# Layer 1's routing: the last five strips settled as one batch beside the first tiles, six early batches, marks copied per strip, and the first plan in pieces

## The chip, the cores and the metric

The kernel runs on one core of a Trainium2 chip. The time is device microseconds of one execution; three executions of the kernel before are given with their median, and one more was taken with the hardware profiler. Engines are called PE (matmul), DVE (vector), ACT (scalar), POOL (GpSimd) and SP (the queue that issues most transfers).

## The reference

Two layers of a metaformer on an image of 2 x 256 channels x 56 x 56. In each layer a spatial mixer (layer 0: attention in 7 x 7 windows; layer 1: two 3 x 3 convolutions with ternary weights, each with batch normalization) is added to the image, and then a mixture of experts is added to every token. Cut to the part that is changed, layer 1's mixture is:

```python
logits = xf @ gate_w + gate_b                 # xf: 6272 tokens, layer-normed, 256 wide; 8 experts
probs = softmax(logits)
top2_vals, top2_idx = lax.top_k(probs, 2)
cw = zeros((N, 8)).at[arange(N)[:, None], top2_idx].add(top2_vals)
for e in range(8):                            # hidden width 512
    h = gelu(xf @ W1[e] + b1[e]); y = h @ W2[e] + b2[e]
    out = out + cw[:, e:e+1] * y
```

## The kernel before

The image is cut into 14 strips of 8 rows. A strip is 3 or 4 groups of 128 tokens (`groups_of`), 49 groups in all, and two strips are 7 groups. Layer 0 computes attention strip by strip, then its expert tiles; layer 1 computes the two convolutions, then the strips of its mixture, then its expert tiles, and at the end the sum of both experts of each token is written out.

**Rows and tiles.** Only the two chosen experts of a token are computed. `routing` gives every (token, expert) pair a place in a scratch tensor `xs` in DRAM, in which each expert has its own stretch of rows. A row is the normed token (256 words) and RW - 256 further words: `R_ID` is the number of the token's first output row, `R_EX` says which expert was its first choice. With these two marks the tile later finds where its results go. POOL scatters the rows, 128 per indirect DMA (L934), two per group: one for each choice. A tile is then 256 rows of one expert: SP loads the rows (`xg`, L1134) and the expert's weights (`w`, L1145, 1154 KB in layer 1), PE transposes the rows (`pt`, L1155), computes the hidden layer (`ph`, L1187) and the result (`py`, L1206), DVE adds the bias (`y`, L1216), and POOL scatters the results to `ys` (L1218). Half tiles of 128 rows take the remainders.

**A strip of layer 1.** `residual` loads `back`, forms x in DVE (L2213), relu in ACT (`nr`, L2216), transposes in PE (`pt`, L2226) and adds in DVE (L2230). `norm` takes the statistics (L744 to L754), scales in ACT (`u`, L767), transposes in PE (`pu`, L815), copies in ACT (`ut`, L818), and multiplies by the gate in PE (`pl`, L827); DVE adds the gate's bias (L836) and so has the logits `lgs`.

**A settling.** `settle(strips)` finds for all groups of a batch of strips the two largest logits (twice `first_max`, L862 to L866), counts (`hots` to `seen`, L887 to L892), has PE count the rows ahead of each within the batch (`rk`, L897 to L900), and turns that into places (`place`, `rowf`, `pos`, L909 to L916). It is a generator: each `yield` ends a step, and after the fourth each further step sends one group. In layer 1 a group that is sent before the tiles begin gets its marks on POOL first: a memset and two copies (L930 to L932). The strips after the ninth get theirs on DVE (L807, L808, L879).

**Plans.** `planning(part)` finds, by DVE on tables, the expert and first row of each tile (`where`), from counts that one matmul sums over the partitions (`counts`, L990, L992). Part 0 is made from the first nine strips alone (`FIRST[1]` is 9): 23 early tiles of 256 rows, whose rows are all known then. Parts 1 and 2, the remaining full and half tiles, are made while the early tiles run. A step of `planning` ends at each `yield`.

**Order.** Inside `manual_schedule` the order on SP, DVE, PE and ACT is the order in which the program emits. `all_strips` emits the strips in passes: in pass i strip i begins, strip i-1 goes on and strip i-2 ends; then the batch that ended is settled up to `rk`, and `send` finishes its places and scatters in the next pass. After the last strip it makes part 0 of the plan in one piece and starts the tiles' generator, which fetches the weights of three tiles; then the tiles begin with the rows of four. Beside the tiles `beside1` is called four times a tile, and each time takes one step of `rest`: of every four calls one goes to `sends` (groups held back), two to `settling` (the last two batches and then the other two plans), and one to nothing. The rows in `u` have eight buffers, `rk`, `pu` and `counts` share two PSUM banks in the strips, and beside the tiles `rk` and `counts` use a bank of `py`.

Of the kernel before, what the change touches and what calls it, by code (L numbers as in the profile page):

```python
# [20 lines left out]
P = 128  # L21
# [31 lines left out]
RW = C + 4  # L53
# [28 lines left out]
ROWS_AHEAD, AHEAD = 4, 3  # L82
UNITS = len(STRIPS) // 2
# [560 lines left out]
def metaformer(ctx: ExitStack, tc: tile.TileContext, a: dict, out: bass.AP, flag):  # L644
# [132 lines left out]
    def routing(layer, wp, tp, ps):  # L777
# [11 lines left out]
        chosen = wp.tile([P, NGR], F32, tag="chosen", name="chosen")  # L789
# [7 lines left out]
        def norm(i, src, late=False):  # L797
# [8 lines left out]
            if layer == 0 or i >= FIRST[1]:  # L806
                eng.memset(row[:, :, R_EX + 1 :], 0.0)  # L807
                eng.tensor_copy(row[:, :, R_ID], ids[:, g0 : g0 + ng])  # L808
# [32 lines left out]
        def settle(strips):  # L841
# [8 lines left out]
            def small(name, shape=(P, n, E), dt=F32):  # L850
                cap, size = max(n, NTT), int(np.prod(shape[1:]))
                t = tp.tile([P, size * cap // n], dt, tag=f"{name}_{cap}", name=name, bufs=1)
                t = t[:, :size]
                if len(shape) == 2:
                    return t
                if len(shape) == 3:
                    return t.rearrange("p (a b) -> p a b", b=shape[2])
                return t.rearrange("p (a b c) -> p a b c", b=shape[2], c=shape[3])
# [14 lines left out]
            at = [chosen[:, t0 : t0 + n], small("at", (P, n))]  # L873
            rest = small("rest")
            first_max(lg, m[0], hot[:, 0], at[0])
            if layer == 0 or strips[0] >= FIRST[1]:
                q = 0
                for u in us:
                    small_eng.tensor_copy(u[:, :, R_EX], at[0][:, q : q + u.shape[1]])  # L879
                    q += u.shape[1]  # L880
# [37 lines left out]
            for t in range(n):  # L918
                if layer == 0 or late:

                    with tc.issue_after(pace[-1]) if pace else nullcontext():
                        cast = nc.vector.tensor_copy(
                            pos[:, :, t0 + t : t0 + t + 1], rowf[:, :, t : t + 1]
                        )
                    if pace:
                        pace[:] = [cast.ins]
                if layer and not late:
                    u = at_of[t][0][:, at_of[t][1], :]
                    with tc.issue_after(spread[-1]) if spread else nullcontext():
                        nc.gpsimd.memset(u[:, R_EX + 1 :], 0.0)  # L930
                        nc.gpsimd.tensor_copy(u[:, R_ID : R_ID + 1], ids[:, t0 + t : t0 + t + 1])
                        nc.gpsimd.tensor_copy(u[:, R_EX : R_EX + 1], at[0][:, t : t + 1])  # L932
                for j in range(TOP):
                    w = nc.gpsimd.indirect_dma_start(  # L934
                        xs[:, :],
                        bass.IndirectOffsetOnAxis(ap=pos[:, j, t0 + t : t0 + t + 1], axis=0),
                        at_of[t][0][:, at_of[t][1], :],
                        None,
                    )
                    apart(f"rows{layer}", w)  # L940
                    if layer:
                        spread[:] = [w.ins]
                    if FIRST[layer] and strips[0] >= FIRST[layer]:

                        disjoint(w, f"late{layer}", f"early{layer}")
                yield
# [386 lines left out]
    BATCHES = [[0], [1], [2], [3], [4], [5, 6], [7, 8], [9, 10], [11, 12], [13]]  # L1333
# [510 lines left out]
    with mid:  # L1844
# [338 lines left out]
        with ExitStack() as both:  # L2183
# [54 lines left out]
            def send(steps, i):  # L2238

                if i >= FIRST[1]:  # L2240
                    if next(steps, steps) is not steps:
                        held.append(steps)
                else:
                    finish(steps)

            def all_strips():

                n = len(STRIPS)
                jobs = {}
                ready = iter(())  # L2250
                for i in range(n + 2):
# [3 lines left out]
                    send(ready, old - 1)  # L2255
# [9 lines left out]
                    steps = iter(())  # L2265
                    if old in jobs:
                        finish(jobs.pop(old))
                        for q in BATCHES[:-2]:
                            if q[-1] == old:
                                steps = settle(q)  # L2270
                    if i == n:
                        plan, n_early = tiles(0)
                        plans1.append(plan)
                        next(experts1)
                    for _ in range(3):
                        next(steps, None)
                    if old == 0:
                        finish(steps)
                    if young in jobs and i < n:
                        next(jobs[young])  # L2280
                    ready = steps
                send(ready, n - 1)
                return n_early

            def settling():

                for q in BATCHES[-2:]:
                    steps = settle(q)
                    for _ in range(4):
                        next(steps)  # L2290
                        yield
                    held.append(steps)
                yield from last_plans()

            def sends():

                at = 0
                while at < len(held):
                    yield from held[at]
                    at += 1  # L2300
# [8 lines left out]
            def rest():  # L2309
# [3 lines left out]
                while True:  # L2313
                    more = next(sending, sending) is not sending
                    yield
                    for _ in range(2):
                        more |= next(others, others) is not others
# [3 lines left out]
                    yield  # L2321
# [197 lines left out]
```

## Time and profile before

| | us |
|---|---|
| median of 3 runs (lowest, highest) | 1740.41 (1736.08, 1745.44) |
| the profiled execution | 1737.13 |
| its span, first to last instruction | 1735.3 |
| strips of layer 1's mixture | 1136 to 1262 |
| first transposition of tile 0 | 1278.2 |
| last products of the last tile | 1670 |

In the profile a group of instructions is named by line, engine and tile, as "PE pl L827"; `out<-in` are the program's names. The chain that ended last is followed back from the last instruction, at each step to what released it. In the order of instructions, a bracket at the end of a line is the idle time of that engine before it and what ended it. PEclk is the clock that PE was granted, as a share of full speed. "SPq" is SP's own queue: L1143 and L1129 read a number of the plan into a register, L1145 issues a weight load.

### The profile page before, as it was taken

The numbers are of one execution on the slowest core, as the hardware profiler recorded it, in microseconds if no ns is written. First come the engines' busy times: TensorE is split into PE (matmuls) and PEld (weight loads), VectorE is DVE, ScalarE is ACT, GpSimd is POOL, SyncE is SP. The second block draws the span as 40 slices with busy tenths as digits, with TensorE's granted clock in tenths as the row PEclk, the third lists the DMA queues.
The fourth block names the chain that finished last, engine by engine and source line by source line (L and its number), as shares of the span: only waits on it lengthen the run. The fifth ranks groups of instructions, "written<-read, shape, count | busy, mean of one in ns | idle before, by whom it ended". The sixth has DMA issues, their size and how long they took to land. (4 is left out here: it accounts for less than half of the span.)

```text
span 1735.3 us, 25573 instructions
## 1 busy us (share of the span) xinstructions
PE 1507.6 (87%) x8445; PEld 1176.0 (68%) x8445; DVE 957.5 (55%) x2620; ACT 692.9 (40%) x1419; POOL 636.8 (37%) x728
## 2 busy tenths in 40 slices
PE   5999998999878788894989879957769999999964
PEld 3555565556557667783768768746658888888852
DVE  3456667466635335885999888777622212111136
ACT  2544443444323324544444263235423334343323
POOL 2111436235333653552333323427715542222210
PEclk9999999999879999996999989955579999999975
DMA  7112334112257769794441000024357777888858
GB/s 241 42 64 90 111 102 145 60 62 80 80 181 248 249 203 322 258 331 176 170 170 70 1 1 0 10 65 141 126 198 274 271 258 262 282 288 288 293 198 317
DMA packets 94157, 291.78 MB, mean 168 GB/s; under 512 B 20151, under 2 KB 35611, under 8 KB 84928
## 3 DMA queue, kind: packets, MB, share of 16 engines
q1 hardware_dynamic: 70384, 231.82, 40.3%
q0 software_dynamic: 19824, 51.82, 7.9%
q10 hardware_dynamic: 3808, 6.42, 1.0%
q8 instruction: 69, 1.13, 0.3%
q14 instruction: 72, 0.59, 0.1%
HBM read 218.55 MB, written 74.20 MB: 169 GB/s over the span
## 5 line engine op out<-in xcount | busy, mean ns | idle before, releaser
L1187 PE MATMUL ph<-ut,w 128*128 128x256 f32 (+1 forms) x1472 | 311.8, 363 | 18.5 <-DMA w<-in_L_experts 10.0
L1216 DVE TENSOR_TENSOR y<-py,w 128x512 f32<-128x512 f32 (+1 forms) x120 | 76.8, 640 | 412.5 <-PE py L1206 341.4
L1206 PE MATMUL py<-w,h 128*128 128x256 f32 x1288 | 300.5, 381 | 3.4 <-DVE y L1216 2.5
L1187 PEld LDWEIGHTS ph<-ut,w 128*128 128x128 f32 x1472 | 251.4, 195 | 49.6 <-DMA w<-in_L_experts 10.3
L1206 PEld LDWEIGHTS py<-w,h 128*128 128x128 f32 x1288 | 244.5, 192 | 37.1 <-DVE y L1216 2.9
L934 POOL DMA_INDIRECT xs<-u,pos x196 | 194.0, 990 | 127.9 <-issue 43.1
L1218 POOL DMA_INDIRECT ys<-y,dest x136 | 137.0, 1008 | 233.0 <-DVE dest L1162 100.4
L1194 ACT ACTIVATE h<-ph,w 128x256 f32<-128x256 f32 (+1 forms) x368 | 162.6, 448 | 119.0 <-PE ph L1187 91.5
L1597 ACT ACTIVATE ex<-sc 112x476 f32<-112x476 f32 (+3 forms) x224 | 116.9, 573 | 177.6 <-PE sc L1587 169.8
L1159 ACT COPY ut<-pt 128x512 f32<-128x512 f32 (+1 forms) x120 | 65.1, 543 | 293.1 <-PE pt L1155 258.2
L1928 PE MATMUL pc<-lo,wq 128*128 128x448 f32 x336 | 131.8, 394 | 5.7 <-DVE lo L1903 5.4
L1617 DVE TENSOR_TENSOR acc<-av,acc 128x238 f32<-128x238 f32 (+3 forms) x224 | 88.1, 408 | 82.9 <-PE av L1607 74.7
L1928 PE MATMUL pc<-hi,wq 128*128 128x448 f32 x336 | 131.0, 392 | 2.5 <-DVE x L1950 1.9
L1607 PE MATMUL av<-ex,vals 112*64 112x238 f32 (+3 forms) x896 | 126.9, 407 | 4.0 <-DVE acc L1617 4.0
L1218 POOL DMA_INDIRECT ys<-y,to x81 | 81.7, 1009 | 121.9 <-DVE dest L1162 63.4
L2071 PE MATMUL pc<-hi,wq 128*128 128x448 f32 (+1 forms) x288 | 102.5, 366 | 18.1 <-ACT hi L2038 9.4
L1578 PE MATMUL sc<-q_im,keys 32*112 32x238 f32 (+3 forms) x896 | 99.2, 423 | 7.9 <-ACT ex L1597 7.8
L2071 PE MATMUL pc<-lo,wq 128*128 128x448 f32 (+1 forms) x288 | 101.8, 363 | 0.2 <-DVE lo L2039 0.2
L1155 PE MATMUL pt<-ident,xg 128*128 128x128 f32 x434 | 71.2, 285 | 33.6 <-DMA xg<-xs 25.5
L1901 POOL TENSOR_TENSOR v<-pad 128x928 f32<-128x928 f32 (+1 forms) x28 | 56.7, 2035 | 103.5 <-ACT pad L1884 59.5
L1607 PEld LDWEIGHTS av<-ex,vals 112*64 112x64 f32 x896 | 57.3, 143 | 53.5 <-issue 30.0
L1155 PEld LDWEIGHTS pt<-ident,xg 128*128 128x128 f32 x434 | 56.5, 148 | 48.8 <-DMA xg<-xs 22.5
(278 smaller groups left out, 2474.5 us busy)
## 6 DMA issues: line engine op xcount, KB each, us to landing
w<-in_L_experts SPq DMA_DIRECT2D x64, 1154.0 KB
w<-in_L_experts SPq DMA_DIRECT2D x56, 641.0 KB
xg<-xs SPq DMA_DIRECT2D x97, 260.0 KB
acc<-in_fresh SPq DMA_DIRECT2D x14, 896.0 KB
got<-ys SPq DMA_DIRECT2D x21, 512.0 KB
got<-ys SPq DMA_DIRECT2D x7, 1024.0 KB
xt<-in_x_tok SPq DMA_DIRECT2D x14, 448.0 KB
rec<-shares SPq DMA_DIRECT2D x28, 224.0 KB
```

The lines of the kernel that those rows point to most:

```text
L934: w = nc.gpsimd.indirect_dma_start(xs[:, :], bass.IndirectOffsetOnAxis(ap=pos[:, j, t0 + t : t0 + t + 1], axis=0), at_of[t][0][:, at_of[t] ...
L1155: nc.tensor.transpose(pt[:, k, i * P : (i + 1) * P], d["xg"][:, i, k * P : (k + 1) * P], ident)
L1187: nc.tensor.matmul(ph[:, :g], w1[:, k, f * P : (f + 1) * P], d["ut"][:, k, :g], start=k == 0, stop=k == KC - 1,)
L1194: nc.scalar.activation(d["h"][:, f, :g], ph[:, :g], AF.Gelu, bias=b1[:, f : f + 1])
L1206: nc.tensor.matmul(py[:, i, :], d["h"][:, f, i * P : (i + 1) * P], w2[:, f, :], start=f == 0, stop=f == NF - 1,)
L1218: o = nc.gpsimd.indirect_dma_start(ys[:, :], bass.IndirectOffsetOnAxis(ap=d["to"][:, i : i + 1], axis=0), y[:, i, :], None, bounds_check=T ...
L1578: nc.tensor.matmul(sc[h // 2][:, h % 2, :nq], keys[g][p, c, tx * TT : (tx + 1) * TT], q_im[p, c, r0:r1, c0:c1], start=True, stop=False,)
L1597: nc.scalar.activation(e[:, :, :nq], sc[j][:, :, :nq], AF.Exp, scale=HD**-0.5)
L1607: nc.tensor.matmul(av[VW * i : VW * (i + 1), :nq], vals[g % 3][:, tx, 2 * c + j, 2 * i : 2 * i + 2, :].rearrange("p a d -> p (a d)"), ex[j ...
L1617: added = nc.vector.tensor_tensor(d, av[:, :nq].rearrange("p (h w) -> p h w", w=c1 - c0), d, ALU.add)
L1928: nc.tensor.matmul(pc[:, :NT], wq[:, k, c, dx * C + o * P : dx * C + (o + 1) * P], part[:, :, k, dx : dx + W], start=m == 0, stop=m == 2 * ...
L2071: nc.tensor.matmul(pc[:, : 2 * ns * W], wq[:, k, c, dx * C + o * P : dx * C + (o + 1) * P], part[:, : 2 * ns, k, dx : dx + W], start=m == ...
```

## The change

- `RW` falls by two words; a row now has 258. `chosen` becomes the second column of a table `marks`, whose first column is filled once from `ids`; in both layers POOL copies both marks for a whole strip in one instruction. Memsets of the two spare words are gone, and so are the copies for the late strips on DVE.
- The batches of layer 1 were [0], [1], [2], [3], [4], [5,6], [7,8], [9,10], [11,12], [13]; the last two were settled beside the tiles. They become [0], [1], [2], [3,4], [5,6], [7,8], and one batch of 18 groups, [9..13], beside the tiles.
- A batch that ends with strip 5 or later is settled in three parts: `first_max` twice in its own pass, the counting and `rk` in the next, places and scatters in the one after.
- Part 0 of the plan is made in pieces of three steps from pass 11 on, and the weights of three tiles are fetched as soon as it is done.
- Beside the tiles the order of steps is one of eight calls: three for sends, three for settling and plans, two for nothing.

```diff
@@ -50,7 +50,7 @@
 NFULL = (TOP * N - E * (G - 1)) // G
 NHALF = (TOP * N + E * (P - 1)) // P - 2 * NFULL
 ROWS = NREG * G
-RW = C + 4
+RW = C + 2
 R_ID, R_EX = C, C + 1
 FAR = 1 << 20
 NEVER = -3e38
@@ -80,6 +80,7 @@
 EARLY = tuple(max(0, (TOP * P * groups_of(n)[0] - E * (G - 1)) // G) for n in FIRST)
 X_FIRST = 3
 ROWS_AHEAD, AHEAD = 4, 3
+PLAN_AT = 11
 UNITS = len(STRIPS) // 2
 FOURS = ((0, 1), (2, 3, 4, 5), (6, 7, 8, 9), (10, 11, 12, 13))
 COMPS4 = 6
@@ -786,7 +787,8 @@
         most = wp.tile([P, TOP, NGR], F32, tag="most", name="most")
         pos = wp.tile([P, TOP, NGR], I32, tag="pos", name="pos")
         wgt = rt.tile([P, TOP, NGR], F32, tag="wgt", name="wgt", bufs=2)
-        chosen = wp.tile([P, NGR], F32, tag="chosen", name="chosen")
+        marks = wp.tile([P, NGR, 2], F32, tag="marks", name="marks")
+        nc.gpsimd.tensor_copy(marks[:, :, 0], ids)
         seen = wp.tile([P, E], F32, tag="seen", name="seen")
         nc.vector.memset(seen, 0.0)
         seen_b4 = wp.tile([P, E], BF16, tag="seen_b4", name="seen_b4")
@@ -803,9 +805,6 @@
             row = tp.tile([P, NTT, RW], F32, tag="u", name="u", bufs=U_BUFS[layer])
             row = rows[i] = row[:, :ng]
             u = row[:, :, :C]
-            if layer == 0 or i >= FIRST[1]:
-                eng.memset(row[:, :, R_EX + 1 :], 0.0)
-                eng.tensor_copy(row[:, :, R_ID], ids[:, g0 : g0 + ng])
             scaled(u, src, rstd, nmr)
             yield
             ut = tp.tile([P, KC, NTT * P], F32, tag="ut", name="ut", bufs=1)
@@ -838,7 +837,7 @@
                 nc.vector.tensor_copy(lg, pl)
             yield
 
-        def settle(strips):
+        def settle(strips, pool=None):
 
 
             t0 = groups_of(strips[0])[0]
@@ -849,7 +848,9 @@
 
             def small(name, shape=(P, n, E), dt=F32):
                 cap, size = max(n, NTT), int(np.prod(shape[1:]))
-                t = tp.tile([P, size * cap // n], dt, tag=f"{name}_{cap}", name=name, bufs=1)
+                t = (pool or tp).tile(
+                    [P, size * cap // n], dt, tag=f"{name}_{cap}", name=name, bufs=1
+                )
                 t = t[:, :size]
                 if len(shape) == 2:
                     return t
@@ -870,13 +871,13 @@
             lg = lgs[:, t0 : t0 + n, :]
             m = [most[:, j, t0 : t0 + n] for j in range(TOP)]
             hot = small("hot", (P, TOP, n, E))
-            at = [chosen[:, t0 : t0 + n], small("at", (P, n))]
+            at = [marks[:, t0 : t0 + n, 1], small("at", (P, n))]
             rest = small("rest")
             first_max(lg, m[0], hot[:, 0], at[0])
-            if layer == 0 or strips[0] >= FIRST[1]:
-                q = 0
+            if layer == 0:
+                q = t0
                 for u in us:
-                    small_eng.tensor_copy(u[:, :, R_EX], at[0][:, q : q + u.shape[1]])
+                    nc.gpsimd.tensor_copy(u[:, :, R_ID:], marks[:, q : q + u.shape[1]])
                     q += u.shape[1]
             nc.vector.scalar_tensor_tensor(rest, hot[:, 0], NEVER, lg, ALU.mult, ALU.add)
             yield
@@ -924,12 +925,12 @@
                         )
                     if pace:
                         pace[:] = [cast.ins]
-                if layer and not late:
-                    u = at_of[t][0][:, at_of[t][1], :]
+                if layer and at_of[t][1] == 0:
+                    u = at_of[t][0]
                     with tc.issue_after(spread[-1]) if spread else nullcontext():
-                        nc.gpsimd.memset(u[:, R_EX + 1 :], 0.0)
-                        nc.gpsimd.tensor_copy(u[:, R_ID : R_ID + 1], ids[:, t0 + t : t0 + t + 1])
-                        nc.gpsimd.tensor_copy(u[:, R_EX : R_EX + 1], at[0][:, t : t + 1])
+                        nc.gpsimd.tensor_copy(
+                            u[:, :, R_ID:], marks[:, t0 + t : t0 + t + u.shape[1]]
+                        )
                 for j in range(TOP):
                     w = nc.gpsimd.indirect_dma_start(
                         xs[:, :],
@@ -1330,7 +1331,7 @@
             except StopIteration as end:
                 return end.value
 
-    BATCHES = [[0], [1], [2], [3], [4], [5, 6], [7, 8], [9, 10], [11, 12], [13]]
+    BATCHES = [[0], [1], [2], [3, 4], [5, 6], [7, 8], [9, 10, 11, 12, 13]]
 
 
     ys = [dram.tile([TOP * N, C], F32, tag=f"ys{i}", name=f"ys{i}", bufs=1) for i in range(2)]
@@ -2235,24 +2236,18 @@
 
             norm, settle, tiles, planning, gates, wgt1, _, sent = routing(1, wp, tp, ps)
 
-            def send(steps, i):
-
-                if i >= FIRST[1]:
-                    if next(steps, steps) is not steps:
-                        held.append(steps)
-                else:
-                    finish(steps)
-
             def all_strips():
 
                 n = len(STRIPS)
-                jobs = {}
-                ready = iter(())
+                jobs, steps = {}, iter(())
+                ready, early = iter(()), None
                 for i in range(n + 2):
                     young, old = i - 1, i - 2
                     if young in jobs:
                         next(jobs[young])
-                    send(ready, old - 1)
+                    finish(ready)
+                    next(steps, None)
+                    ready, steps = steps, iter(())
                     if young == 0:
                         next(jobs[young])
                     if i < n:
@@ -2262,42 +2257,46 @@
                         next(jobs[young])
                     if i == n:
                         next(jobs[young])
-                    steps = iter(())
                     if old in jobs:
                         finish(jobs.pop(old))
-                        for q in BATCHES[:-2]:
+                        for q in BATCHES[:-1]:
                             if q[-1] == old:
                                 steps = settle(q)
-                    if i == n:
-                        plan, n_early = tiles(0)
-                        plans1.append(plan)
-                        next(experts1)
-                    for _ in range(3):
-                        next(steps, None)
-                    if old == 0:
-                        finish(steps)
+                                next(steps)
+                                next(steps)
+                                if old < 5:
+                                    next(steps)
+                                    ready, steps = steps, iter(())
+                                if old == 0:
+                                    finish(ready)
+                    if i == PLAN_AT:
+                        early = planning(0)
+                    if i >= PLAN_AT and not plans1:
+                        try:
+                            for _ in range(3):
+                                next(early)
+                        except StopIteration as end:
+                            plan, n_early = end.value
+                            plans1.append(plan)
+                            next(experts1)
                     if young in jobs and i < n:
                         next(jobs[young])
-                    ready = steps
-                send(ready, n - 1)
                 return n_early
 
             def settling():
 
-                for q in BATCHES[-2:]:
-                    steps = settle(q)
-                    for _ in range(4):
-                        next(steps)
-                        yield
-                    held.append(steps)
+                steps = settle(BATCHES[-1], tp1)
+                for _ in range(4):
+                    next(steps)
+                    yield
+                held.append(steps)
                 yield from last_plans()
 
             def sends():
 
-                at = 0
-                while at < len(held):
-                    yield from held[at]
-                    at += 1
+                while not held:
+                    yield
+                yield from held[0]
 
             def last_plans():
 
@@ -2311,14 +2310,13 @@
                 yield
                 sending, others = sends(), settling()
                 while True:
-                    more = next(sending, sending) is not sending
-                    yield
-                    for _ in range(2):
-                        more |= next(others, others) is not others
+                    more = False
+                    for it in (sending, others, others, None, sending, others, sending, None):
+                        if it:
+                            more |= next(it, it) is not it
                         yield
                     if not more:
                         return
-                    yield
 
             plans1, held = [], []
             gating = gates()
```

## The prediction

> **What bounds the kernel now.** I read the page first, then the busy time by stages, then the chain that ended last around the edit, then the order of instructions on POOL, PE and DVE there.
>
> ```profile
> span 1735.3 us, 25573 instructions
> PE 1507.6 (87%) x8445; PEld 1176.0 (68%) x8445; DVE 957.5 (55%) x2620; ACT 692.9 (40%) x1419; POOL 636.8 (37%) x728
> ```
>
> The profiled execution took 1737.13 us: 1.8 us lie around the span. The median shown is 1740.41, 3.3 above it. 87% of PE is a mean over stages; the edit is in layer 1's strips and in the start of its tiles.
>
> ```profile
> core 0: us, PE busy (x) PEld busy (x) DVE busy (x) ACT busy (x) POOL busy (x), PEclk, DMA share, GB/s
> 1136.00:1262.00 126.00, 93.97 (x439) 80.36 (x439) 90.56 (x362) 60.53 (x119) 74.31 (x153) 0.53 0.36 114
> 1262.00:1278.00 16.00, 0.04 (x2) 0.00 (x0) 4.25 (x21) 0.00 (x0) 0.00 (x0) 0.50 0.64 252
> 1278.00:1300.00 22.00, 21.81 (x109) 19.02 (x110) 4.76 (x25) 9.32 (x17) 5.85 (x6) 0.91 0.56 207
> 1300.00:1440.00 140.00, 140.00 (x691) 123.16 (x690) 33.54 (x139) 49.33 (x99) 69.04 (x70) 1.00 0.76 262
> ```
>
> To be seen: 126 us of strips in which no engine is full and PE runs at half clock; 16 us in which PE does nothing; then tiles with PE 100% busy. A microsecond saved before 1278 is kept through the PE-bound tiles.
>
> ```profile
> 1258.86 3.16 PE pl L827 x14
> 1262.09 0.18 DVE counts L992
> ...
> 1265.89 0.12 SPq L1143
> ...
> 1266.48 0.35 SPq L1145
> ...
> 1269.08 0.34 SPq L1145
> ...
> 1270.33 7.81 DMA xg<-xs
> 1278.19 1.97 PE pt L1155 x8
> 1280.15 4.51 PE ph L1187 x16
> ...
> 1285.10 3.46 PE ph L1187 x16
> ```
>
> The gap in order: the plan on DVE (1262.1 to 1265.9), three weight loads of 1154 KB issued from 1266.5 to 1269.4, then the rows of tile 0, issued 1270.3 and landed 1278.1. From the first weight issue to that landing are 11.7 us for 3 x 1154 + 260 KB, about 320 GB/s.
>
> ```profile
> 1250.59 0.11 POOL L930 MEMSET u<- 128x2 f32 x1
> 1250.63 0.19 POOL L931 COPY u<-ids 128x1 f32<-128x1 f32 x1
> 1250.75 0.18 POOL L932 COPY u<-chosen 128x1 f32<-128x1 f32 x1
> 1251.21 0.99 POOL L934 DMA_INDIRECT xs<-u,pos  x1 [0.28 <-issue]
> 1252.51 0.96 POOL L934 DMA_INDIRECT xs<-u,pos  x1 [0.30 <-issue]
> ```
>
> One group on POOL: 2.88 us from one memset to the next, of which two scatters with their pauses are 2.55. POOL is nearly continuous from 1169 and finishes the early rows at 1253.5, so today the scatter is covered by the strips.
>
> ```profile
> 1224.71 0.23 PE L897 MATMUL rk<-hots,before_w 128*128 128x56 bf16 x1 [1.79 <-DVE hots L887]
> 1226.79 1.12 PE L815 MATMUL pu<-ident,u 128*128 128x128 f32 x4 [0.68 <-issue]
> 1233.63 1.23 DVE L2230 TENSOR_TENSOR x<-pt,back 128x1024 f32<-128x1024 f32 x1 [1.66 <-PE pt L2226]
> ```
>
> A pair of strips takes 16.6 to 18.6 us (starts of the four-group L2230: 1164.1, 1182.7, 1199.8, 1216.5, 1233.6, 1251.0). PE waits for a settling's `hots`, DVE for PE's `pt`: a chain over both.
>
> **The change, part by part.** I call the pass that begins with L2230 of strip i-1 "pass i"; passes 10, 12, 14 begin at 1216.5, 1233.6, 1251.0.
>
> (1) Fewer settlings in the strips. [3] goes into [4]: pass 5 lasted 10.0 us (1172.7 to 1182.7) with DVE's settling after L836; without it PE's `pt`, done at 1181.0, ends the pass: -1.5, and -0.2 in pass 6 (DVE loses four place instructions, 0.8, and gains 0.6 by larger ones). [9,10] leaves pass 12: 16 DVE instructions, 3.7 us, counted in (4).
>
> (2) Settlings [5,6] and [7,8] in pieces. `hots` to `seen` (4 instructions, 0.85) and `rk` go to the next pass, `place` to `pos` (0.9) to the one after. Pass 8 loses 0.85 on DVE and PE its 1.8 wait; pass 9 gains the 0.85 ahead of L2213, but its PE work starts earlier with two free `pu` banks: -1.5 for the pair. In pass 10 `place` now sits before L2213, where DVE is the chain: +0.9, which cancels the 0.85: the pair 10-11 gains 0.9.
>
> (3) The plan in pieces, passes 11 to 13. 20 DVE instructions, 3.8 us in the chain above. The order of the changed kernel shows the price of the first piece: `counts` (L990) stands on PE behind `pt` of strip 11, and DVE's L992 to L1024 stand before L2230 of that strip. So DVE waits for `counts`, and L2230 with all behind it starts 2.4 us after `pt` instead of at once; PE's next `pu` takes the bank of `counts` and waits 0.3. Costs 2.4, no cover; (2) less (3) makes the pair 10-11 1.5 longer. The second piece (4 instructions, 1.1) takes part of the place of [9,10]; the third (1.6) fits in the 1.66 in which DVE waited for PE; without that cover it costs 1.6.
>
> (4) Pass 12: DVE 3.1 (L2230, statistics) + 0.9 (`place`) + 1.6 + 0.2 + 1.1 = 6.9; PE's `pt` then ends it at 7.9 instead of 8.8; pass 13 7.9 instead of 8.5: -1.5. Sum at pass 14: -1.7 - 1.5 + 1.5 - 1.5 = -3.2: it begins at 1247.8 and the strips, 11 us later, end near 1258.7.
>
> (5) POOL. Memset and two copies per group go; one copy per strip stays, about 0.45 with its pause. A batch of seven groups: 7 x 2.55 + 0.45 = 18.3. [5,6] starts 4.4 after pass 10 (1213.3), at 1217.7, ends 1236.0. [7,8] is a pass later: 4.1 after pass 12 (1231.9), at 1236.2; ends 1254.5, a microsecond later than before in spite of the fewer instructions. From the end of the last scatter to the rows' issue I take 2.2 (the chain's scatter of 1218.19 landed 3.15 after its start) to 4.1 (layer 0: 489.7 to 493.8): issue at 1256.7 to 1258.6. Layer 0's first rows took 2.8 from issue to use: 1259.5 to 1261.4.
>
> (6) Weights. `where` is ready just before pass 14, so the loads issue at about 1248. Queued on SP before them are only the strips' loads of `back`, the last of them done by then; behind them only the rows. The trace's layer 0 would have the rows 2.8 after their issue. The Trainium skill, "DMA: Bandwidth & Descriptors", section "Queues, rings and completion order", says descriptors of one issuing queue are consumed in ring order on each engine: the rows cannot pass the weights. By that rule 1248 + 11.7 = 1259.7, plus 2 for the 0.6 MB of scatter in the same time at 320 GB/s: 1261.5. Both ways end near 1261.4; I take this for tile 0, against 1278.2: -16.8. The PE gap is then 2.7 us.
>
> (7) In the tiles. One settling of 18 groups for two of 7 and 4: 19 `rk` matmuls on the bound PE instead of 13, wider; from the rows of 0.2 and their overlap I estimate +0.5 to +1.5, take +1. DVE (24% busy from 1300 to 1440) covers its 24 wider instructions; if not, `y` is late, and `py` has two banks. POOL has 2 ys and on average 3 xs a tile, 5 x 1.29 = 6.4 of 7.35 us; PE sees it only when the five `y` buffers are used up. The sends end near tile 15, before rows of the late plan are fetched at tile 19.
>
> (8) Rows of 258 instead of 260 words, layer 0's memsets and copies gone from POOL and DVE, some early DVE and SP instructions reordered, Exp one tile earlier: 0, hidden by attention and PE-bound tiles; bounds -2 and +2, as POOL loses some 28 x 0.15 and a swapped load at the start may come later.
>
> Sum: -16.8 + 1 = -15.8, about -16: 1721 on the profiled execution's own time, 1724.4 on the median's.
>
> **A rule against the gain.** PE is at 0.50 in the strips, and tile 0's `ph` took 4.51 against 3.46. "TensorE: Matmul & The Clock Gate", Part 1, says half clock holds until PE has been busy through a window of about 3.4 us. By the trace alone the 1.05 warm-up is paid as before; by the rule a 2.7 us gap may keep what the strips have, which is half clock, so the same. But if fewer stalls in the strips let a window fill, `pl` (6.2 of each pair) and the transposes would halve: up to 3 us per pair over some three pairs, -9. No run shows it; I take 0 and keep -9 as the lower end.
>
> **Rivals.**
> A, 60%: as above, -11 to -20.
> B, 20%: the gap becomes a transfer wait. Weights and scatter slow each other; if the last scatters land 6 to 9 us later (their 0.6 MB and the 3.5 MB at 200 to 250 GB/s, rates that other stages show, in place of 320), tile 0 starts near 1269: -8, 1732. For it: nothing in the trace shows this mix. Against: 320 GB/s was reached.
> C, 10%: the clock rule's upside, or POOL sooner: -20 to -27, about 1717.
> D, 7%: slower. The row of xs shrinks to 1032 bytes, no longer a multiple of 16. If writing and reading such rows cost three times as much, the later tiles, where DMA runs at 0.84 share and 288 GB/s, become transfer-bound: there a full and a half tile in 11.1 us move 390 KB of rows; 780 KB more at 288 GB/s is 2.7 us per pair, less 1.8 of spare, over 18 pairs +16, and as much at tile 0 and in layer 0: 1752. It decides from about double cost. Against: rows of 1040 also start off most boundaries.
> E, 3%: the start waits for something not seen (a buffer or bank freed only at the strips' end): the gap stays, -2.
>
> **How the numbers follow.** 0.5% (8.7 us) is about what a measurement of this kernel can tell from no change. Faster by more: A, C and nearly half of B, 0.79. Within: the rest of B, E, 0.13. Slower: D and a small rest, 0.08. Range: A with its bounds, most of B and the edge of C, with the 4 us by which runs of before scatter: 1714 to 1736.
>
> **What would show it.** Tile 0's `pt` (L1155) near 1261 with 2 to 5 us of PE idle before it; weights issued near 1248; L2230 of strip 11 late by about 2.4 with DVE waiting for `counts`; POOL's last early scatter near 1254.5, without memsets; tiles at 7.35 us as before. Wrong if tile 0 starts after 1268 (B, E), if PEclk in the strips rises above 0.6 (C), or if tiles grow beyond 7.4 us (D).

## The result, and the profile after

The changed kernel takes 1746.41 us in the median of 22 runs (1739.43 to 1755.85), the kernel before 1740.57 us on the same chip (22 runs): a ratio of 1.0039, 95% interval [1.0024, 1.0054]. It is slower by 0.4%, where 16 us less had been forecast. The profiled execution took 1753.02 us, near the upper end of the runs.

The page of the changed kernel:

```profile
span 1751.2 us, 25389 instructions
PE 1512.9 (86%) x8442; PEld 1180.2 (67%) x8442; DVE 948.4 (54%) x2546; ACT 690.0 (39%) x1419; POOL 621.9 (36%) x627
```

DVE and POOL have less to do, as planned (POOL 101 instructions fewer). The busy time by stages, which answers to the table of before:

```profile
core 0: us, PE busy (x) PEld busy (x) DVE busy (x) ACT busy (x) POOL busy (x), PEclk, DMA share, GB/s
1148.50:1293.40 144.90, 91.67 (x425) 79.64 (x425) 85.14 (x328) 58.89 (x117) 63.13 (x71) 0.51 0.39 129
1293.40:1315.40 22.00, 22.00 (x115) 19.17 (x116) 5.50 (x21) 9.30 (x17) 2.25 (x3) 0.89 0.48 166
1315.40:1455.40 140.00, 139.14 (x684) 122.29 (x683) 30.94 (x121) 47.70 (x99) 73.31 (x78) 1.00 0.77 262
```

There is no row for a gap any more: the strips are followed at once by tiles with PE full. But the strips take 144.9 us, with PE busy for no more time than before. On PE, at the seam:

```profile
1290.35 3.16 PE L826 MATMUL pl<-gate,ut 128*128 128x8 f32 x14 [0.26 <-ACT ut L817]
1293.36 1.95 PE L1156 MATMUL pt<-ident,xg 128*128 128x128 f32 x8
1295.13 1.22 PE L1188 MATMUL ph<-ut,w 128*128 128x256 f32 x2
```

The last logits (`pl`) run into tile 0's `pt` with no idle time; before, 16.15 us lay between. Those 16 us were gained, and more than 16 were lost inside the strips. To compare runs I count from the first L2231 (before: L2230) of layer 1's strips, since that point itself moves from run to run: 1139.8 before, 1148.5 here, and 1147.8 in a kernel below (e3) whose code up to there is that of before. From it, tile 0 starts at 138.4 us before and at 144.9 now. That difference, 6.5 us, agrees with the 0.4% by which the medians differ.

Where the strips lose it, the waits between 1148 and 1294 us tell (engine and line, who ended the wait; total, times, longest):

```profile
ACT ut L817 <- remote: 28.2, 6, 9.4
...
DVE counts L993 <- remote: 9.8, 1, 9.8
...
DVE x L2231 <- remote: 7.9, 2, 4.5
```

"remote" stands where the signal that ended a wait has no recorded instruction ending next to it. The strips before have no such wait. All are waits for PE, whose instructions stand in the trace microseconds earlier. One of them in order of time:

```profile
1247.35 2.35 PE L2227 MATMUL pt<-ident,nr 128*128 128x128 f32 x8 [1.11 <-issue]
...
1248.27 0.96 POOL L935 DMA_INDIRECT xs<-u,pos  x1 [0.30 <-issue]
1249.23 0.20 POOL L931 COPY u<-marks 128x6 f32<-128x6 f32 x1
...
1249.49 0.21 PE L991 MATMUL counts<-seen_b,all_w 128*128 128x8 bf16 x1
1249.71 0.98 POOL L935 DMA_INDIRECT xs<-u,pos  x1 [0.28 <-issue]
...
1256.05 0.96 POOL L935 DMA_INDIRECT xs<-u,pos  x1 [0.30 <-issue]
1257.00 0.21 POOL L931 COPY u<-marks 128x8 f32<-128x8 f32 x1
1257.74 0.17 DVE L993 COPY counts<-counts 128x8 f32<-128x8 f32 x1 [9.79 <-remote]
...
1258.06 0.88 PE L814 MATMUL pu<-ident,u 128*128 128x128 f32 x3 [8.35 <-DVE counts L993]
```

PE's eight `pt` and the `counts` behind them would end at 1249.7 by their usual durations; PE's signals, which the trace records by themselves, come at 1257.68 and 1257.72. DVE, which needs `counts`, stands still for 9.8 us, and PE then for 8.35. POOL meanwhile scatters on, one every 1.27 us, from 1239.2 to 1257.0, and the hold-up ends with POOL's last scatter. So it is with every run of 14 scatters in the strips: POOL scatters from 1177.6 to 1195.7, from 1208.3 to 1226.4, from 1239.2 to 1257.0 and from 1265.0 to 1283.0, and the waits of this kind (for L2231, `ut` and `counts`) end at 1194.0 and 1196.8, at 1225.4 and 1228.3, at 1257.7, and at 1279.4 to 1285.0. The first wait of each group begins 8 to 11 us after the run's start; PE's signals then come singly, and the last of the waits ends 0.7 to 2 us after the run.

### The profile page after: what moved, and what is told of

Same layout as the page of the kernel before. It is cut to its first block, busy times and chain, and to the rows that moved or that the text cites. A ratio compares the mean times of both kernels' runs of the same rounds, so it can differ in the third digit from the quotient of the medians.

```text
span 1751.2 us, 25389 instructions
## 1 busy us (share of the span) xinstructions
PE 1512.9 (86%) x8442; PEld 1180.2 (67%) x8442; DVE 948.4 (54%) x2546; ACT 690.0 (39%) x1419; POOL 621.9 (36%) x627
## 5 line engine op out<-in xcount | busy, mean ns | idle before, releaser
L826 PE MATMUL pl<-gate,ut 128*128 128x8 f32 x392 | 68.3, 304 | 25.7 <-ACT ut L817 13.9
L826 PEld LDWEIGHTS pl<-gate,ut 128*128 128x128 f32 x392 | 65.7, 254 | 34.3 <-ACT ut L817 17.2
```

Of the source, the lines that this page charges most:

```text
L826: nc.tensor.matmul(pl[:, t, :], ut[:, k, t * P : (t + 1) * P], gate[:, k, :], start=k == 0, stop=k == KC - 1,)
```

## The experiments

Times are medians, each beside the kernel before on the same chip; the ratio is that of the comparison and need not be the quotient of the two medians. Five sets of runs were made. In the first and the last the kernel before took 1740.1 and 1743.7 us, as in the result; in the second, third and fourth 1720.2, 1720.8 and 1722.1. They ran on chips 14, 10, 13, 13 and 8; the chip of the result is not on record.

| kernel | us | before | ratio, 95% interval |
|---|---|---|---|
| e1_paced | 1732.1 | 1740.1 | 0.9934 [0.9902, 0.9966] |
| e2_before_rows258 | 1742.9 | 1740.1 | 1.0002 [0.9982, 1.0021] |
| e3_before_dense | 1758.6 | 1740.1 | 1.0078 [1.0042, 1.0114] |
| e4_copy_per_group | 1734.3 | 1740.1 | 0.9964 [0.9939, 0.9989] |
| b1_paced_early | 1709.7 | 1720.2 | 0.9931 [0.9906, 0.9957] |
| b2_paced | 1709.6 | 1720.2 | 0.9933 [0.9905, 0.9961] |
| b3_paced_late_plan | 1714.3 | 1720.2 | 0.9969 [0.9952, 0.9986] |
| e5_half_rows | 1708.3 | 1720.2 | 0.9913 [0.9890, 0.9937] |
| after_2 (the changed kernel) | 1709.0 | 1720.8 | 0.9925 [0.9900, 0.9950] |
| e5_half_rows_2 | 1705.5 | 1720.8 | 0.9914 [0.9886, 0.9942] |
| b2_paced_2 | 1706.9 | 1720.8 | 0.9920 [0.9900, 0.9940] |
| after_3 (the changed kernel) | 1700.7 | 1722.1 | 0.9871 [0.9843, 0.9899] |
| e5_half_rows_3 | 1702.4 | 1722.1 | 0.9898 [0.9865, 0.9931] |
| b2_paced_3 | 1710.0 | 1722.1 | 0.9919 [0.9888, 0.9949] |
| b5_paced_both | 1707.7 | 1722.1 | 0.9923 [0.9897, 0.9948] |
| e5_half_rows_4 | 1750.8 | 1743.7 | 1.0043 [1.0007, 1.0079] |
| b5_paced_both_4 | 1730.5 | 1743.7 | 0.9922 [0.9894, 0.9950] |

**First set: the pace of the scatters, the rows, or the order.** Of the changed kernel, only the pauses on POOL are put back (e1), or a shorter one (e4); of the kernel before, only the row width (e2) or only the missing pauses (e3) is changed.

e1:

```diff
-                if layer and at_of[t][1] == 0:
+                if layer and not late:
+                    u = at_of[t][0][:, at_of[t][1], :]
...
+                        nc.gpsimd.memset(u[:, R_ID:], 0.0)
+                        nc.gpsimd.tensor_copy(u[:, R_ID : R_ID + 1], marks[:, t0 + t, 0:1])
+                        nc.gpsimd.tensor_copy(u[:, R_EX : R_EX + 1], marks[:, t0 + t, 1:2])
+                elif layer and at_of[t][1] == 0:
...
```

> The changed kernel, but the marks of layer 1's early rows are written per group again, by a memset and two small copies on POOL between the scatters, as in the kernel before; rows stay 258 words wide, and batches, plan and weights stay as changed. Theory (density): PE is held up while POOL issues more than about eight scatters with no pause between them, 1.27 us each; with the three small operations a scatter comes every 1.44 us and the hold-ups of 3 to 9 us in the strips go: passes of 8.2 to 8.8 us throughout, tile 0 right behind the last logits or up to 4 us later, and about 13 to 18 us less than the changed kernel: 1728 to 1733. Rival (rows): rows of 1032 bytes do it; then nothing changes, 1746 +- 3. Rival (order): the pieces of settlings and plan do it; nothing changes either.

e4 has one copy of both marks there: `nc.gpsimd.tensor_copy(u[:, R_ID:], marks[:, t0 + t, :])`.

> The changed kernel with the copy of the two marks per group instead of per strip in the early batches: one small POOL operation between two pairs of scatters, about 2.75 us per group. Density: most or all of the hold-ups go, 10 to 18 us less than the changed kernel: 1728 to 1736; if the pause has to be longer, they stay in part, about 1740. Rows and order: nothing changes, 1746 +- 3.

e2, on the kernel before:

```diff
-RW = C + 4
+RW = C + 2
...
-                        nc.gpsimd.memset(u[:, R_EX + 1 :], 0.0)
+                        nc.gpsimd.memset(u[:, R_ID:], 0.0)
```

> The kernel before with one thing of the change: rows of 258 words instead of 260. The memset of the two pad words becomes one of the two mark words, which the copies then fill, so POOL has as many operations as before. Density: nothing, 1740 +- 3, no hold-ups of PE in layer 1's strips. Rows: hold-ups as in the changed kernel and 10 us or more on top of 1740. Order: nothing.

e3, on the kernel before:

```diff
-                if layer and not late:
-                    u = at_of[t][0][:, at_of[t][1], :]
+                if layer and not late and at_of[t][1] == 0:
+                    u, k = at_of[t][0], at_of[t][0].shape[1]
...
+                        nc.gpsimd.memset(u[:, :, R_EX + 1 :], 0.0)
+                        nc.gpsimd.tensor_copy(u[:, :, R_ID], ids[:, t0 + t : t0 + t + k])
+                        nc.gpsimd.tensor_copy(u[:, :, R_EX], at[0][:, t : t + k])
```

> The kernel before with one thing of the change: in layer 1's early batches the memset and the two copies are made once per strip instead of once per group; rows stay 260 words, batches and plan as before. Density: POOL now issues a scatter every 1.27 us in runs of up to 14, PE is held up 3 to 9 us near the end of each, passes of 12 us and more appear, and the time rises by 8 to 20 us: 1748 to 1760. Rows and order: nothing, 1740 +- 3.

The pace decides. e3, with nothing but the pauses gone, is slower than before and has the waits in its strips:

```profile
ACT ut L818 <- remote: 33.2, 4, 9.7
DVE x L2230 <- remote: 4.1, 1, 4.1
```

Its passes reach 12.8, 14.1 and 12.9 us where before had at most 10.0, and its gap ahead of tile 0 is still there, so tile 0 starts 160.7 us after the first L2230. e2 has none of these waits in the strips and the time of before: rows of 1032 bytes are as good as rows of 1040. (Its copies wait for its memset, so its scatters come only every 1.6 us or so; that narrow rows are not needed for hold-ups is shown by e3, which has the wide ones.) e1 has none either, and its strips end 116.4 us after the first L2231. Its own POOL operations wait for each other, though (the copies write the words that the memset has just written; a scatter then comes every 1.6 us or so instead of before's 1.46 to 1.49), so that POOL ends its last early scatter at 122.0 and tile 0 starts only at 126.6. By the medians 8 us of 16 are gained.

e4 shows that there is no sharp limit. Its mean spacing is 1.38 to 1.43 us; its runs of 14 pass without a hold-up, but in its run of 28, 1.39 us apart from 1223.8 on, the first waits begin between 1242 and 1246, after 14 to 16 scatters:

```profile
ACT ut L817 <- remote: 15.1, 3, 8.3
DVE lgs L835 <- remote: 8.8, 2, 7.4
DVE x L2235 <- remote: 4.7, 2, 3.2
```

At about 1.30 us (the strip's copy included) the first wait of a run begins after 7 to 10 scatters (the changed kernel, e3), at 1.39 after 14 to 16, at 1.46 to 1.50 not in 28 (before; b5_paced_both_4 below). That is how a backlog would behave that is worked off at one scatter in roughly 1.5 us (a rough estimate from these three); no run shows the backlog itself.

**Second set: a better pace, sooner scatters, the plan, and half the bytes.** b2 has e1's two copies, but the memset goes to an unused tile (`nc.gpsimd.memset(idle, 0.0)`), so that none waits for another; b1 is b2 with [3] and [4] as two batches; b3 is b2 with the plan in one piece, three passes later:

```diff
-PLAN_AT = 11
+PLAN_AT = 14
...
-                            for _ in range(3):
+                            for _ in range(9):
```

e5 is the changed kernel, dense as it is, with half rows: in layer 1's early scatters the first half of each row is left out.

```diff
+                nc.vector.tensor_scalar(pos2[:, :, t0 : t0 + n], rowf, 2.0, 1.0, ALU.mult, ALU.add)
...
+                    cut = RW // 2 if layer and not late else 0
                     w = nc.gpsimd.indirect_dma_start(
-                        xs[:, :],
-                        bass.IndirectOffsetOnAxis(ap=pos[:, j, t0 + t : t0 + t + 1], axis=0),
-                        at_of[t][0][:, at_of[t][1], :],
+                        xs[:, :].rearrange("r (h c) -> (r h) c", h=2) if cut else xs[:, :],
...
+                            ap=(pos2 if cut else pos)[:, j, t0 + t : t0 + t + 1], axis=0
...
+                        at_of[t][0][:, at_of[t][1], cut:],
```

> The changed kernel with three independent small POOL operations between two pairs of scatters (two copies of a mark, a memset of an unused tile: 1.46 us a scatter as in the kernel before), and batch [3,4] split into [3] and [4] again, so that POOL has work sooner. Density: no hold-ups in the strips, POOL's last early scatter about 114 us after the strips' first L2231 where the paced kernel has 122, tile 0 at about 119 where it has 126.5 and the kernel before 138.4: about 1724 (1720 to 1729). If hold-ups in the strips stay: 1740 and over.

> As the last, with the batches of the changed kernel ([3,4] together): POOL starts that batch a strip later. Tile 0 about 121 to 123 us after the first L2231, so 1726 to 1732. If the split of [3,4] is worth nothing, equal to the last.

> As the last, but the first plan is made in one piece after the last strip's logits pass has begun (three passes later), as in the kernel before, and the weights are issued after it. If the plan in pieces is what closes the gap ahead of tile 0, about 8 to 12 us come back: 1737 to 1742, with weights issued within a few us of the strips' end. If the gap was closed by something else, equal to the last.

> The changed kernel, dense as it is, but layer 1's early scatters carry only the second half of each row (129 words and the marks, 516 bytes instead of 1032); the first halves are left out of the rows. Same number of scatters, of descriptors' rows and of POOL instructions, half the bytes. If bytes or the transfers' own time hold PE up: no hold-ups, about 1725. If it is the rate of issuing (descriptors, semaphores): hold-ups as in the changed kernel, about 1746.

All four are faster than before by 5 to 15 us, but the times themselves had been expected 14 us higher or more, since the kernel before takes 1720 here. And none of them has a single wait of the kind above, in no stage: not even in layer 0, where all of the first set and the kernel before have had them between 570 and 645 us. There b2 issues 45 scatters, of rows and of results, 1.28 us apart (573.1 to 629.5) with no hold-up. So e5 tells nothing yet of bytes. What the set does tell: b1 and b2 are equal, so splitting [3,4] is worth nothing (POOL's last early scatter ends at 120.5 and 118.8). And the plan in pieces is worth 4.7 us by the medians: in b3 the weights are issued from 119.2 us on, counted as above, after the last logits at 114.6, and tile 0 starts at 131.8; in b2 at 105.1 and 124.1. I had expected 8 to 12 to come back. A likely reason that it is less: in b2 the rows, issued at 121.3, have to wait for POOL's scatters, which end at 118.8, whatever the weights do.

**Third and fourth set: the changed kernel where PE isn't held up.**

> The changed kernel once more, beside the other three of this set on one chip. In the last set the kernel before took 1720 us instead of 1740 and none of its companions showed a hold-up of PE, not even in layer 0's dense runs of scatters, so the hold-ups may belong to some chips and not to others. If the chip of this set has them (the kernel before near 1740): 1746. If not (the kernel before near 1720): no hold-ups, 14 to 18 us less than the kernel before, as predicted.

> The kernel before with its profile from this chip. Near 1740 with hold-ups of PE between 570 and 645 us in layer 0, or near 1720 without them.

> The changed kernel with half rows in layer 1's early scatters (the first halves of the rows are left out), beside the full rows of the changed kernel on one chip. If this chip holds PE up: by bytes, about 1722 to 1727 (no hold-ups in the strips); by the rate of issuing, about 1746. If it doesn't: equal to the changed kernel or up to 4 us less, as POOL and the rows' transfers are no slower.

> The changed kernel with three small POOL operations between pairs of scatters. On a chip that holds PE up: 0.993 of the kernel before, so 1727 to 1730 where that takes 1740. On one that doesn't: 0.993 too, and slower than the changed kernel itself by 2 to 5 us, as POOL ends its early scatters later.

The kernel before took 1719.87 us in its profiled execution. The changed kernel is faster by 0.75% in the third set and by 1.3% in the fourth. Its stages (after_2, then before_2; the columns are those above):

```profile
1127.70:1249.70 122.00, 93.08 (x425) 80.36 (x425) 85.42 (x330) 59.48 (x117) 63.39 (x71) 0.51 0.45 149
1249.70:1271.70 22.00, 21.67 (x116) 18.78 (x117) 5.53 (x20) 9.26 (x17) 2.26 (x3) 0.92 0.56 190
```

```profile
1124.70:1246.80 122.10, 90.82 (x433) 78.03 (x433) 88.84 (x357) 59.21 (x117) 74.19 (x153) 0.54 0.37 118
1246.80:1263.80 17.00, 0.08 (x2) 0.00 (x0) 4.24 (x21) 0.00 (x0) 0.00 (x0) 0.50 0.65 248
```

The same program takes 144.9 us for what takes 122.0 here. The strips end (last `pl`) 116.6 us after the first L2231, and 145.0 with the hold-ups: they cost 28.4 us, of which 5.4 would have been spent waiting for tile 0's rows in any case. The scatters are as dense here, every 1.27 us. The half rows change nothing (0.9914 and 0.9898 against 0.9925 and 0.9871), and the paced kernel (0.9920, 0.9919) is not told apart from the changed one in the third set; in the fourth it looks slower, with intervals that just overlap. Such small differences can't be read across sets: the changed kernel itself has 0.9925 and 0.9871 in two sets on one chip, with intervals that don't meet.

> The changed kernel beside the next three on one chip. Where the kernel before takes about 1740: 1746, with hold-ups; where it takes about 1720: 1708, without.

> The changed kernel with half rows in layer 1's early scatters (first halves left out). On a chip with hold-ups: by bytes, none in the strips and about 1724; by the rate of issuing, as the changed kernel, 1746. On one without: as measured, about 15 us less than the kernel before.

> The changed kernel with three small POOL operations between pairs of early scatters. On a chip with hold-ups: none in the strips, 1726 to 1732. Without: about 0.992 of the kernel before.

b5 is b2 with three memsets of one word ahead of each pair of scatters in layer 0's late batches:

```diff
+                if layer == 0 and late:
+                    with tc.issue_after(spread[-1]) if spread else nullcontext():
+                        for k in range(3):
+                            nc.gpsimd.memset(idle[:, k : k + 1], 0.0)
...
-                    if layer:
+                    if layer or late:
                         spread[:] = [w.ins]
```

The last lines note the last scatter, behind which the memsets are to be issued.

> As the last, and three small memsets between the pairs of scatters of layer 0's late batches too, which go beside that layer's first tiles. On a chip with hold-ups: those between 570 and 645 us go in part (scatters of rows alternate there with scatters of results, which keep 1.27 us), 5 to 15 us less than the last: 1712 to 1725. Without hold-ups: equal to the last, or 1 to 3 us more where rows come later.

It equals b2 here.

**Fifth set: half the bytes where PE is held up.**

> The changed kernel with half rows in layer 1's early scatters (first halves left out). On a chip with hold-ups (the kernel before near 1740): by bytes, none in the strips and about 1724; by the rate of issuing, hold-ups of 3 to 9 us as in the changed kernel, 1746. On a chip without (near 1720): about 15 to 17 us less than the kernel before.

> Pauses between pairs of row scatters in layer 1's early and layer 0's late batches. On a chip with hold-ups: none in the strips, fewer between 570 and 645 us, 1712 to 1725 where the kernel before takes 1740. On a chip without: 0.992 of the kernel before, as measured.

With half the bytes in each early scatter the hold-ups are what they were:

```profile
ACT ut L818 <- remote: 28.2, 6, 8.8
DVE x L2236 <- remote: 9.9, 3, 4.6
DVE counts L998 <- remote: 9.8, 1, 9.8
```

The time is that of the changed kernel, 1.0043 of before. So it is not the bytes; it is how often scatters of 128 rows are issued. Whether the scatters or their rows count was not separated, since each has 128. b5 has no such wait in its strips, its passes are within 0.2 us those of b2 in the second set, and it takes 0.9922 of before. Its memsets in layer 0 did nothing: they fit into the pause of 0.30 us that lies between two scatters anyway, the spacing there stayed at 1.27 to 1.30 us, and that layer's hold-ups stayed too (34.9 us of "remote" waits between 500 and 700 us; 28.6 in the kernel before). Whether a true pause there would bring the 20 us by which the kernel before differs between sets was not tried. Since those memsets do nothing, b5 shows b2's pace where PE is held up: at 0.992 in both kinds of sets the paced kernel beats the one before throughout, and the changed kernel (1.0039) where PE is held up.

## Why the prediction was wrong

**The step that failed is (5), as to the pace.** It took the memset and copies of each group as pure cost to POOL, "a batch of seven groups: 7 x 2.55 + 0.45 = 18.3", and gave the denser scatters no price on other engines. Where the result was measured they cost PE 28.4 us in the strips (whether the recording of the trace has a part in that is open; see the end). The rows of before that the prediction itself showed (2.88 us a group, 2.55 of it scatters) held the pauses that mattered. Layer 0 of the same trace held the warning, hold-ups of up to 7.3 us in runs of 8 to 14 scatters at 1.28 to 1.31 us (waits of before between 500 and 700 us):

```profile
DVE y L1216 <- remote: 17.2, 3, 7.1
...
ACT ut L1159 <- remote: 7.3, 1, 7.3
```

The prediction takes no account of them. None of the rivals had this mechanism: D ended on the right side, but with the rows' width, which e2 and e3 rule out.

The other steps can be read from after_2 against before_2, where nothing is held up. Passes are the times from one L2231 to the next.

- (1) Pass 5 went from 10.0 to 8.5 us and pass 6 from 8.6 to 8.1: -2.0, forecast -1.7.
- (2), (3) Passes 8 and 9 together -2.2 (forecast -1.5); passes 10 and 11 +0.7 (forecast +1.5), with the longer pass 11, 9.5 us, where the forecast put the wait for `counts`.
- (4) Passes 12 and 13 -2.1 (forecast -1.5). The strips end 116.6 us after the first L2231 instead of 122.1: -5.5, forecast -3.2 by pass 14.
- (5) as to POOL's own time: the last early scatter ends at 113.9, forecast 114.7 (1254.5 less 1139.8).
- (6) Weights are issued from 104.9 on (forecast 108), tile 0 starts at 122.0 (forecast 121.6), -17.1 against before_2 (forecast -16.8). The way there differs: the PE gap is 5.4 us instead of 2.7, because the strips end sooner while the rows don't. In the chain that ended last (after_2; start, us, what):

```profile
1240.64 6.20 DMA xs<-u,pos
...
1248.09 3.00 DMA xg<-xs
```

The last scatter takes 6.2 us to land where the prediction took 3.15 from one of before. Rival B's mechanism, a scatter slowed by the weights' transfer beside it, fits, at 3 us instead of 6 to 9: three scatters issued while the weights are on their way take 6.7 to 7.0 us to land (after_2, b2), three with none on their way 2.4 to 4.0 (before_2, b3). Tile 0's own rows take 2.7 from issue to use and those of the second tile, in the chain above, 3.0, near layer 0's 2.8; they are issued after the weights' 11.7 us would be over, so the rule on ring order was not put to the test. That tile 0 comes within 0.4 us of the forecast is in part luck: 5.4 us pass from POOL's last scatter to the rows' issue where 2.2 to 4.1 had been taken, and the forecast had used the later end of its range.
- (7) From tile 0 to the end: 457.5 and 455.4 us (after_2, after_3) against 454.2, and 457.9 against 457.1 in the first pair of profiles: +0.8 to +3.3, forecast +1. In that pair the changed kernel has three hold-ups in the tiles too (2.1 to 4.5 us, between 1371 and 1418), where the kernel before has none.
- (8) Layer 0 and the convolutions: the first L2231 is at 1127.7 and 1124.0 against 1124.7, no difference to be seen. Rival C did not come: PEclk stays at 0.51 in the strips, and full clock comes 3.6 us after tile 0 begins.

Altogether 12 and 21 us less where 16 had been forecast, in two sets in which PE isn't held up, and 6 us more where it is. The mechanism of the change was read rightly; its side effect on PE was not seen.

## What to carry to other kernels

Small operations between POOL's scatters may be spacers that another engine lives on. Before making a stream of indirect DMAs denser, look in every stage of the trace for engines that stop, with no signal to explain it, while such a stream runs, and price the new stream by them. Work can be moved off POOL by fewer scatters rather than closer ones (not tried here). Measure on more than one chip when the effect is below 2%, and see whether the trace holds all of its signals before a stop is put down to the hardware alone.

## What the runs showed of the hardware

- In the first and the last set, a long run of POOL's indirect DMAs, 128 rows each and 1.27 to 1.30 us apart, held PE up after 7 to 10 of them until the run ended. Pauses that bring the mean to 1.46 to 1.50 us end that. Half the bytes per row (516 instead of 1032) change nothing. The Trainium skill's "SBUF — State Buffer", section "SBUF: two separate sides", says that engine ports and DMA ports of SBUF are disjoint and that PE never waits there on anyone; that the bytes don't matter agrees with it, so the place is likely another one, which no run here shows.
- SP is slowed in the changed kernel's last hold-up too, DVE and ACT are not (L2231 on four groups takes 1.23 us there as in after_2, `ut` of three groups 0.48). The three weight loads (start, us, what), first in the changed kernel's hold-up, then in after_2:

```profile
1275.69 5.71 SPq L1146 DMA_DIRECT2D w<-in_L_experts  x3
```

```profile
1232.55 3.18 SPq L1146 DMA_DIRECT2D w<-in_L_experts  x3
```

  Of SP's 21 instructions between 1272 and 1284 us, six take 0.69 to 0.71 us, where the same instructions take 0.02 to 0.5 in after_2, and PE's signals of that hold-up, at 1279.30, 1280.72, 1282.85 and 1285.02, lie two and three times 0.71 apart. It looks as if SP's instructions and PE's signals had to wait for turns of 0.71 us. Why, stays open.
- It belongs to some sets of runs and not to others: in the profiles of the second to fourth set there is no such wait with the same programs, and the kernel before takes 20 us less. Two chips had it (14 and 8) and two not (10 and 13, the latter in two sets), and none was seen both ways; whether it is the chip or its condition at the time was not shown.
- One rival stands untested: that the recording of the trace has a part in it. The eight traces with hold-ups have lost signals: 14361 to 15391 are recorded, against 20166 to 20248 in the twelve without. In the changed kernel's, PE's signals are complete from 840 to 1080 us, where POOL scatters nothing (124 of 124), and not beside the scatters from 1294 us on (348 of 413). A wait whose signal is lost is put down to "issue", so the length of the passes is the surer sign of a hold-up. Every execution on record has a recorded span and clock, so no run here tells whether a kernel that is not recorded is held up.
